# A macaron block (feed-forward, attention, feed-forward): the row maxima of head pairs 0 and 1 are found in one pass, pair 0 is attended two key blocks at a time, and some small steps change places

## The chip, the cores and the metric

The kernel runs on one core of a Trainium2 chip. The metric is the device time of one execution in microseconds (us). Below, PE is TensorE (matrix products), DVE is VectorE, ACT is ScalarE, POOL is GpSimd and SP is SyncE, whose queue issues the DMAs. PSUM, the memory that PE writes, has eight banks of 128 x 512 fp32 values.

## The reference

The input x has 2048 tokens of width 512. All products are in fp32.

```python
x = x + 0.5 * ffn(layernorm(x), gate, up, down)       # first feed-forward
x = x + attention(layernorm(x), w_qkv, w_out)         # 16 heads of 32, causal
x = x + 0.5 * ffn(layernorm(x), gate, up, down)       # second, with the same weights

# ffn:  W = LUT[4-bit code] * scale (4096 wide);  inter = gelu(x @ Wg.T) * (x @ Wu.T);  out = inter @ Wd.T
# attention, per head:  softmax(q @ k.T / sqrt(32) + causal mask) @ v;  then out @ w_out.T + b_out
```

## The kernel before, in words

The order of the work is written out by hand. Each engine carries out its instructions in the order in which the Python code emits them; semaphores between the engines follow from which tile each instruction reads and writes. PSUM is split into seven banks that are handed out as they come free (`ps_one`) and one for long accumulations (`ps_acc`). So a matrix product waits when its operand is late, or when no bank has been emptied.

The two feed-forward parts use Strassen-like schemes: seven products in place of eight, on sums of blocks, and in the second part a second level inside each. The first part dequantizes the weights and keeps them in DRAM; the second fetches them.

Attention works on pairs of heads. A head is 32 wide, so the queries and keys of four heads lie in one tile of 128 partitions, `qT` and `kT`: pair 0 in partitions 0 to 63, pair 1 in 64 to 127 (`quadrant`, which gives each head its 32 rows). A product of 32 rows uses a quarter of PE's rows, and products that lie in different quarters can run side by side.

A pair needs two passes. The first, `maxima(p)`, finds the largest score of each query, 40 steps of one 128-query tile against up to 512 keys (the last, diagonal, block of each tile is 128 to 512 wide). A step is one product per head (`pm`, L1208), and a reduction by DVE for each (L1220, or L1216 with the mask on a diagonal block). At the end of each group `g` of 512 queries the negated maxima are split into three bf16 parts by POOL (L1231) and turned into rows by PE (`row`, L1244), which ACT copies to `mrow` (L1245).

The second pass, `attend(p, width)`, again has 40 steps: 128 keys against 512 queries, or fewer on the diagonal. A step puts the maxima into a bank (`ps`, L1359, three bf16 rows), adds the scores of both heads (L1368), exponentiates them on ACT (L1393), and two steps later multiplies them with the values (`av`, L1280). The sums of each two steps' exponentials (L1417) are multiplied with ones to give the denominators, also at L1280. On a diagonal block DVE adds the mask to the first head's scores in PSUM (L1383); the second head's are copied out by ACT (L1386), masked by POOL (L1387) and exponentiated after that (L1395).

Normally `attend(p, 1)` runs in step with `maxima(p + 1)`: two heads' `ps` and the next pair's two `pm` fill the four quarters of PE. Two places are different. The maxima of pair 0 run before, with nothing beside them but the projections that fill the gaps (`pqk` L1124, `pv` L1141), one whole projection after every few steps. The last pair, 7, has no maxima behind it; its queries and keys are copied by DMA to the other half of the tile too, and `attend(7, 2)` takes two steps at once, one from each half, so that four `ps` run side by side.

While `attend(7)` runs, the layer norms for half of the second feed-forward are spread over its last group: `Norm(...).steps()` is a list of ten steps (two of moments on DVE, with the scales on POOL at the end of the second; four normalizations on DVE, L149; four transposes on PE, L155), and a tuple of numbers says after which of the 16 steps each is emitted.

The second feed-forward goes through 56 pairs of products for each half of the tokens (`pair`, seven slots each, L747), then the down products (`down`, `piece(i, q)`, L878): seven products `i` for each of two token groups `q`, slipped between the pairs. Products 1, 6, 7, 4 add up in one bank, 5 and 3 in another, 2 has its own; ACT takes a copy after 1, 6 and 5 (L901), and DVE adds the bank to the residual after the others (L887). Between the halves the class `Later` loads eight token tiles (`xl`, two buffers), normalizes them on ACT (L954), transposes them on PE (`pt_later`, L962) and copies them out. After the very last pair the remaining down products are emitted with the sums, gelus and gates that they need.

## Time and profile before

| | |
|---|---|
| median of 3 runs | 3151.17 us (3149.62 to 3152.65) |
| profiled execution | 3148.55 us; its span from first to last instruction 3146.7 us |
| PE busy | 3106.7 us, 99% of the span |
| DVE, ACT, POOL busy | 2054.1, 1046.7, 1532.9 us |
| last projections and tiles before the maxima of pair 0 | 1187.6 to 1203.4 us of the span |
| maxima of pair 0, with 12 projections between | 1203.4 to 1284.7 us |
| attention of pair 0 with the maxima of pair 1, and 8 projections | 1284.7 to 1385.2 us |
| attention of pair 7 (two steps at a time) | 1952.8 to 2037.1 us |
| last products | 3108.9 to 3142.8 us |

The profile's page gives busy shares by engine and slice, the chain of work that ended last, and groups of instructions by source line. In the timeline a row is: start, duration, engine, line, operation, output tile, input tiles, shapes, and xN for N equal instructions in a row; in brackets the idle time of the engine before it and what ended it. One fp32 product of the program is two matmuls of the profile.

### The profile page before, as it was taken

The page shows a single profiled execution, that of the slowest core. Times are in us where ns is not written, and L with a number is a line of the kernel's source. Part 1 is how long each engine was busy: PE and PEld are TensorE (multiplying, and loading weights), DVE is VectorE, ACT ScalarE, POOL GpSimd, SP SyncE. Part 2 cuts the span into 40 slices and gives each one's busy share as a digit, 9 for nine tenths or more (in the row PEclk, how much of TensorE's full clock was granted, in tenths as well). Part 3 has the DMA queues.
Part 4 walks back from the last instruction along what each step waited for, and adds up shares of the span by engine and source line. Part 5 has one row for each costly group of instructions (what it writes and reads, how often), then busy time and mean ns, then how long its engine had stood idle before and what let it go on. Part 6 is the DMA issues. An engine that isn't in the chain of part 4 may idle for free.

```text
span 3146.7 us, 45156 instructions
## 1 busy us (share of the span) xinstructions
PE 3106.7 (99%) x16592; PEld 2005.8 (64%) x16592; DVE 2054.1 (65%) x3182; ACT 1046.7 (33%) x2070; POOL 1532.9 (49%) x1529
## 2 busy tenths in 40 slices
PE   8999999999999999999999999999999999999999
PEld 4556565656555565444335434478888888888887
DVE  7566666666665655655564566687666777666676
ACT  5111111121111122355553456543333343333332
POOL 3757584857667572456664467522232223223221
PEclk9999999999999999999999999999999999999999
DMA  4223222212122220000000000064444445444442
GB/s 140 90 81 114 83 81 84 97 61 97 67 91 85 83 84 24 5 14 9 12 9 7 29 20 11 1 199 132 125 135 128 123 130 170 119 124 128 127 125 64
DMA packets 261293, 260.21 MB, mean 83 GB/s; under 512 B 21216, under 2 KB 225616, under 8 KB 257104
## 3 DMA queue, kind: packets, MB, share of 16 engines
q1 hardware_dynamic: 261072, 257.33, 25.2%
q8 instruction: 131, 2.15, 0.3%
q14 instruction: 90, 0.74, 0.1%
HBM read 176.28 MB, written 79.92 MB: 81 GB/s over the span
## 4 chain that ended last, share of the span: by engine, by line
PE 93%; DVE 3%; POOL 1%; ACT 1%; issue 1%; DMA 1%; SPq 0%; ACTq 0%; POOLq 0%; DVEq 0%
PE po L439 12%; PE pu L340 12%; PE d_f L747 12%; PE pg L340 12%; PE av L1280 7%; PE pod_f L878 7%; PE pm L1208 6%; PE f_f L747 6%; PE pqk L1124 4%; PE pof_f L878 3%; PE e_f L747 3%; PE ps L1359 2%; PE pv L1141 2%; PE pp L1161 2%; PE poe_f L878 2%; PE ps L1368 1%
## 5 line engine op out<-in xcount | busy, mean ns | idle before, releaser
L1393 ACT ACTIVATE pt<-ps 128x512 f32<-128x512 f32 (+3 forms) x608 | 288.1, 528 | 180.8 <-PE ps L1368 118.6
L1208 PE MATMUL pm<-kT,qT 32*128 32x512 f32 (+3 forms) x1280 | 332.4, 572 | 0.0
L1220 DVE TENSOR_REDUCE parts<-pm 128x1 f32<-128x512 f32 x384 | 246.5, 685 | 129.3 <-PE pm L1208 129.0
L747 PE MATMUL d_f<-ys_f,ring 128*128 128x256 f32 x1216 | 319.8, 384 | 6.1 <-DVE o_f L780 5.7
L1417 POOL TENSOR_TENSOR sum<-pt,pt 128x512 f32<-128x512 f32 (+1 forms) x225 | 265.6, 1200 | 95.6 <-ACT pt L1393 88.6
L1368 PE MATMUL ps<-qT,kT 32*128 32x512 f32 (+3 forms) x1280 | 278.3, 536 | 0.0
L747 PEld LDWEIGHTS d_f<-ys_f,ring 128*128 128x128 f32 x1216 | 227.1, 190 | 53.2 <-DVE o_f L780 21.3
L439 PEld LDWEIGHTS po<-wd,inter 128*128 128x128 f32 x1024 | 194.8, 190 | 77.2 <-issue 54.9
L801 DVE TENSOR_TENSOR o_f<-o_f,o_f 128x1024 f32<-128x1024 f32 x128 | 203.6, 1601 | 61.2 <-ACT o_f L786 56.5
L439 PE MATMUL po<-wd,inter 128*128 128x256 f32 x1024 | 241.1, 379 | 0.0
L340 PE MATMUL pg<-xT_f,w 128*128 128x512 f32 x512 | 239.1, 595 | 1.2 <-ACT u L379 1.2
L340 PE MATMUL pu<-xT_f,w 128*128 128x512 f32 x512 | 238.0, 593 | 0.0
L893 POOL TENSOR_TENSOR xq<-xq,d_f 128x512 f32<-128x512 f32 x48 | 63.6, 1324 | 311.2 <-DVE xq L887 230.3
L453 POOL TENSOR_TENSOR xq<-xq,d 128x512 f32<-128x512 f32 x124 | 161.9, 1316 | 92.0 <-DVE xq L447 55.8
L893 POOL TENSOR_TENSOR xq_second<-xq_second,d_f 128x512 f32<-128x512 f32 x45 | 61.5, 1367 | 277.2 <-DVE xq_second L887 212.3
L1280 PE MATMUL av<-pt,vals 128*32 128x256 f32 (+1 forms) x2432 | 191.5, 370 | 2.4 <-ACT both L1302 2.3
L439 PEld LDWEIGHTS po<-wd,s 128*128 128x128 f32 x768 | 145.7, 190 | 57.7 <-issue 38.9
L394 POOL TENSOR_TENSOR u<-u,u 128x512 f32<-128x512 f32 x64 | 81.7, 1277 | 206.7 <-ACT u L391 205.9
L439 PE MATMUL po<-wd,s 128*128 128x256 f32 x768 | 181.5, 379 | 0.0
L801 POOL TENSOR_TENSOR o_f<-o_f,o_f 128x1024 f32<-128x1024 f32 x44 | 119.2, 2709 | 123.9 <-ACT o_f L786 122.8
L340 PE MATMUL pg<-xsum,w 128*128 128x512 f32 x384 | 177.9, 592 | 0.0
L1280 PEld LDWEIGHTS av<-pt,vals 128*32 128x32 f32 x2432 | 53.0, 108 | 195.8 <-issue 167.9
(225 smaller groups left out, 6460.8 us busy)
## 6 DMA issues: line engine op xcount, KB each, us to landing
wd_f<-kept SPq DMA_DIRECT2D x112, 256.0 KB
kept<-wd SPq DMA_DIRECT2D x8, 1792.0 KB
xq<-in_x SPq DMA_DIRECT2D x16, 256.0 KB
pk<-in_gate_codes SPq DMA_DIRECT2D x16, 256.0 KB
sc<-in_gate_scales SPq DMA_DIRECT2D x32, 128.0 KB
pk<-in_up_codes SPq DMA_DIRECT2D x16, 256.0 KB
sc<-in_up_scales SPq DMA_DIRECT2D x32, 128.0 KB
pk<-in_down_codes SPq DMA_DIRECT2D x16, 256.0 KB
```

Source lines behind the costliest of these rows:

```text
L340: nc.tensor.matmul(ps, lhsT=a[:, j, :], rhs=b[:, j, :], start=(j == 0), stop=(j == 1))
L439: nc.tensor.matmul(ps[:, j, :], lhsT=a[i][:, k, bass.ts(2 * q + j, P)], rhs=b[i][:, k, :], start=(k == 0), stop=(k == 1),)
L453: adder.tensor_tensor(dst, dst, other, ALU.add)
L747: nc.tensor.matmul(ps[:, k, :], lhsT=fa[k][y], rhs=fb[k][y], start=first and k == 0, stop=True, skip_group_check=True,)
L801: sums.append(lambda: eng.tensor_tensor(dst, dst, other, ALU.add))
L878: nc.tensor.matmul(ps[:, j, :], lhsT=a[:, k, bass.ts(2 * q + j, P)], rhs=wd[:, PLACE[i], k, :], start=new and j == k == 0, stop=True, skip ...
L1208: nc.tensor.matmul(ps[a][:, :n], lhsT=q[r, bass.ts(4 * g + i, P)], rhs=k[r, kb * 512 : kb * 512 + n], start=True, stop=True,)
L1220: nc.vector.tensor_reduce(most, scores, AX.X, ALU.max)
L1280: nc.tensor.matmul(dst_, lhsT=lhsT, rhs=rhs, start=kw.get("start", False), stop=True, skip_group_check=True)
L1368: nc.tensor.matmul(ps[a][:, off:], lhsT=k[r, bass.ts(c, P)], rhs=q[r, g * 512 + off : (g + 1) * 512], start=False, stop=True,)
L1393: nc.scalar.activation(pt[:, a, plain[a] :], ps[a][:, plain[a] :], AF.Exp, scale=scale)
L1417: eng.tensor_tensor(s[:, a, off_2:], one[:, a, off_2:], other[:, a, off_2:], ALU.add)
```

## The change

Seven things, in the order of the code.

1. Last down products (`piece`, `down`, the end of `second_ffn`): for the last group, products 1 and 2 of both token groups come first, then 6, 5, 7, 3, 4 of each. For `q == 1` the copy after product 1 and the add after product 2 go; the bank is added to the residual at once. The sums, gelus and gates are placed anew between them: product 3 of the group before now follows product 5 directly.
2. `Later`: each transpose of the token tiles is emitted one slot earlier, with its load and the next normalization (the last transpose stays). One pair of sums in the second half moves one slot up.
3. `maxima(0)` and `maxima(1)` run zipped: a step has four `pm`, in four quarters, and four reductions. `split` has four buffers.
4. The fill is cut into units of one product (`pqk`) or a quarter of a `pv`; `take` says how many units follow a step. The prologue has two projections in place of four; the zipped pass takes all the rest and six of the eight projections of the second group of heads, and the last two are spread over `attend(0)`. Some of them use the free `ps_acc` bank. The bias of the values is added by ACT (copy) and POOL, and `kT` of the second group is written by ACT, both on DVE before.
5. Pair 0 joins pair 7 in `DOUBLE`: `attend(0, 2)` takes two steps at once. For that two DMAs copy pair 0's queries and keys into the other half of two spare tiles, and its maxima rows are made for both halves (eight transposes in place of four, two copies by ACT). Its divisions are done as pair 7's are (reciprocals on DVE, products on POOL, no DMAs), and the first head's half of each sum by DVE.
6. For both pairs in `DOUBLE` the mask of the second head's diagonal block is also added by DVE in PSUM, without the copy, the POOL mask and the extra exponential.
7. In `attend(7)` the second moments and scales of the second normed block are emitted after step 9 in place of 4, and its normalizations and transposes up to two steps later.

```diff
+DOUBLE = (0, NPAIR - 1)
 ...
-                orders = [(1, 2, 6, 5, 7, 3, 4)] * 2 if final else [DOWN, late]
+                order = [(i, q) for q, r in enumerate((DOWN, late)) for i in r]
+                if final:
+                    order = [(i, q) for i in (1, 2) for q in range(2)]
+                    order += [(i, q) for q in range(2) for i in (6, 5, 7, 3, 4)]
 ...
-                place = min(2 * i, 13)
-                at(0, 54 + place // 7, place % 7, call(later.transpose, i))
+                place = 53 * 7 + 6 + 2 * i
+                at(0, place // 7, place % 7, call(later.transpose, i))
 ...
-            at(1, 2, 3, *second[2:])
+            at(1, 2, 2, *second[2:])
 ...
-                    pieces.pop(0)()
-                    for f in sums:
-                        f()
-                    for piece in (pieces.pop(0), pieces.pop(1)):
-                        piece()
-                    for f in gelus + gated + down_sums[:2]:
-                        f()
-                    for piece in (pieces.pop(0), pieces.pop(0)):
-                        piece()
-                    for f in down_sums[2:]:
-                        f()
-                    for piece in pieces:
-                        piece()
+                    for part in (
+                        [pieces.pop(0)] + sums,
+                        [pieces.pop(0) for _ in range(3)] + gelus + gated,
+                        [pieces.pop(0)] + down_sums[:2],
+                        [pieces.pop(0) for _ in range(2)] + down_sums[2:],
+                        pieces,
+                    ):
+                        for f in part:
+                            f()
 ...
+            copies = [an.tile([P, S], F32, tag="attnT", name=f"copy{i}", bufs=3) for i in range(2)]
+            mcopy = [an.tile([P, D], F32, tag="xn", name=f"mcopy{i}").bitcast(BF16) for i in range(2)]
 ...
-                        for i in range(2):
-                            nc.vector.tensor_tensor(
-                                vals[...], ps[:, i, :], bv_sb[...], ALU.add)
+                        if half == 0:
+                            nc.scalar.copy(both, ps[0])
+                        for i in range(2):
+                            eng, src = (nc.gpsimd, both) if half == 0 else (nc.vector, ps[0])
+                            eng.tensor_tensor(both[:, i, :], src[:, i, :], bv_sb[...], ALU.add)
 ...
-                                halves = (p % 2,) if p + 1 < NPAIR else (0, 1)
+                                halves = (0, 1) if p in DOUBLE else (p % 2,)
 ...
+                            for a in range(2 if p in DOUBLE else 1):
+                                own = ps[a][:, off : off + P]
+                                nc.vector.tensor_tensor(own, own, mask_k, ALU.add)
+                            if p not in DOUBLE:
+                                plain[1] = off + P
+                                ...
 ...
-            for piece in qk[:4]:
+            for piece in joined(qk[:2]):
                 piece()
                 for step in norms[:3]:
                     step()
                 del norms[:3]
-            fill = qk[4:6] + v[:2] + qk[6:8] + v[2:]
-            for n, (matmuls, rest, diagonal) in enumerate(maxima(0)):
+            def second_group():
+                nc.sync.dma_start(out=wqk_sb, in_=wqk[1])
+                for src, dst in zip((qT, kT), copies):
+                    nc.sync.dma_start(out=dst[64:, :], in_=src[0][:64, :])
+            for piece in qk[2:6] + v[:2] + qk[6:] + [second_group] + v[2:] + following[:6]:
+                ...

+            for n, pair in enumerate(zip(maxima(0), maxima(1))):
                 for a in range(2):
-                    matmuls(a)
+                    for matmuls, _, _ in pair:
+                        matmuls(a)
                 for a in range(2):
-                    rest(a, now)
+                    for _, rest, _ in pair:
+                        rest(a, now)
                 now += 1
+                take = 3 if n < 3 else 4 if n == 39 else 1 if n in (10, 11, 22, 23, 32) else 2
+                for f in units[:take]:
+                    f()
 ...
-                0: lambda: spread(project_qk(1)),
+                0: lambda: [[], following[6], following[7], []],
 ...
-                            after = ((0, 1, 4, 5, 6, 6, 7, 8, 9, 10), (3, 4, 9, 10, 11, 12, 12, 13, 14, 15))[tb][i]
+                            after = ((0, 1, 4, 5, 6, 6, 7, 8, 9, 10), (3, 9, 11, 11, 12, 12, 13, 13, 14, 15))[tb][i]
 ...
-                ahead = maxima(p + 1) if p + 1 < NPAIR else iter(())
+                ahead = iter(()) if p in DOUBLE else maxima(p + 1)
 ...
-                for steps in attend(p, 2 if p + 1 == NPAIR else 1):
+                for steps in attend(p, 2 if p in DOUBLE else 1):
```

## The prediction

> **What bounds the kernel now.** I read the page first, then the timeline of PE from the last projections to the end of pair 7, then the waits of PE in the stages that the diff touches.
>
> ```profile
> PE 3106.7 (99%) x16592; PEld 2005.8 (64%) x16592; DVE 2054.1 (65%) x3182; ACT 1046.7 (33%) x2070; POOL 1532.9 (49%) x1529
> ...
> 1209.83 1.13 PE L1208 MATMUL pm<-kT,qT 32*128 32x512 f32 x4
> 1210.89 3.70 PE L1124 MATMUL pqk<-xT_a,wqk_wv 128*128 128x512 f32 x8
> ...
> 1324.75 0.39 PE L1359 MATMUL ps<-wo_bo,ones_b 3*128 3x512 bf16 x1
> 1324.75 0.69 PE L1208 MATMUL pm<-kT,qT 32*128 32x512 f32 x1
> ...
> 1325.93 0.64 PE L1280 MATMUL av<-pt,vals 128*32 128x256 f32 x8
> 1326.50 0.39 PE L1359 MATMUL ps<-wo_bo,ones_b 3*128 3x512 bf16 x1
> ...
> 1982.05 0.40 PE L1359 MATMUL ps<-wo_bo,ones_b 3*128 3x512 bf16 x4
> 1982.28 1.03 PE L1368 MATMUL ps<-qT,kT 32*128 32x512 f32 x8
> 1983.23 0.64 PE L1280 MATMUL av<-pt,vals 128*32 128x256 f32 x8
> 1983.69 0.61 PE L1280 MATMUL av<-sum,ones_f 128*32 128x256 f32 x8
> 1984.12 0.61 PE L1280 MATMUL av<-pt,vals 128*32 128x256 f32 x8
> 1984.67 0.40 PE L1359 MATMUL ps<-wo_bo,ones_b 3*128 3x512 bf16 x4
> ```
>
> PE is the bound nearly everywhere, so a gain is either PE time that goes or one of its few waits. But busy isn't full: from start to start, a step of `pm` takes 1.06 us (1209.83 to 1210.89) with two of four quarters in use, and a step of pair 0's attention beside `pm` 1.18 + 0.57 us (1324.75, 1325.93, 1326.50). Pair 7's double step of four `ps` takes the same 1.18 us (1982.05 to 1983.23) for two steps' scores, and 2.62 us in all. So half of PE is unused in the maxima of pair 0, and the last pair shows what filling it gives.
>
> ```profile
> PE pt_f L155 <- ACT xn_f L146: 11.6, 4, 8.7
> PE d_f L747 <- DVE o_f L780: 5.7, 5, 2.3
> PE ps L1359 <- ACT pt L1393: 3.3, 3, 2.0
> PE pt_later L962 <- ACT xl L954: 2.9, 5, 1.4
> ...
> 2015.86 0.75 PE L155 MATMUL pt_f<-ident,xn_f 128*128 128x128 f32 x4 [1.30 <-DVE xn_f L149]
> 2019.31 0.26 PE L1359 MATMUL ps<-wo_bo,ones_b 3*128 3x128 bf16 x1 [1.98 <-ACT pt L1393]
> 2020.47 1.08 PE L1280 MATMUL av<-pt,vals 128*32 128x256 f32 x8
> ```
>
> These are PE's waits (total, times, longest): the 3.3 us and the two rows below lie in pair 7, the 2.9 us between the halves of the second feed-forward; the first row is the kernel's start, which stays. In the last row the same `av` that took 0.64 us takes 1.08: the granted clock is 0.88 in the 20 us from 2020.
>
> **The change part by part.** Built, both programs have the same PE products except 16 more row transposes; the PE sum is about which run side by side.
>
> *Attention of pair 0.* Two full steps are 1.75 and 2.22 us now (1324.75, 1326.50, 1328.72), 3.97 together, against 2.62 for a double step: 1.35 saved, 12 times. For the diagonal the timeline gives 2.21 + 1.49 against 2.61 (512 and 384 wide) and 1.66 + 1.01 against 2.09: 1.09 and 0.58, four times each. Together 16.2 + 4.4 + 2.3 = 22.9 us. The projections (8 x 3.63 us) and the rows of pair 1 (4 x 0.34) only move into the stage before.
>
> *Maxima of pairs 0 and 1.* Pair 1's `pm` go into the two free quarters. Price: 1.06 us a full step as now, if four overlap as two do. Pair 7's four fp32 `ps` take 0.95 us after their bf16 rows, so I take 0 for that. Here a rule speaks against the change. The Trainium skill, "TensorE: Matmul & The Clock Gate", in "Part 3: Packing small matmuls", gives four row tiles of 32 x 512 a measured speedup of 3.07, not 4. By the rule a full step's 0.855 us of streaming (1242.96 to 1245.73 is three steps, less 0.2 of entry) would become 1.11, over 24 full and 16 partial steps (34 in full widths) an estimated +8.8 us. The row of this trace is the nearer case; I keep 0, and 8.8 as the other end. What does cost is that now every step stands between fills: 19 blocks of `pm` today become 40, and each entry from a 128-row product costs 1.06 - 0.855 = 0.2 us, so 21 x 0.2 = +4.3 us.
>
> *Who keeps up.* PE in the new stage: 80 units x 0.907 = 72.6, `pm` 28 x 1.06 + 4 x (0.85 + 0.63 + 0.42) = 37.3, seven tile transposes x 0.63 and six row groups x 0.34 = 6.4, in all 116 us. DVE: 96 reductions at 0.635 (eight in 5.08 us) = 61, diagonals 16 x (0.645 + 0.515 + 0.385 + 0.25) = 29, moments and small ones 5, in all 95 us; that is why the bias of the values and `kT` leave it. Per full step it is 2.54 against 2.88 us. ACT gets 14 x 0.59 for projections, 8 x 0.57 for values, POOL 16 x 0.77 for the bias (the 128x256 row of L272) beside 16 x 1.26 of residual bias: both under half. Banks: four `pm`, at times an open projection. When the next step starts 2.9 us later, DVE has emptied two or three, so four are free. The cover goes once: the moments of the second normed block (4 x 0.8 us) now stand on DVE after the third step and, behind them, a reciprocal that waits for ACT; the next step's reductions queue behind it, and the fourth `pm` of the first full step waits for its bank, 1.5 us. Also the first `pm` waits for `kT` off ACT (0.59 us, partly under a transpose): 0.4. Today's 0.9 us of waits for `xn_a` there go.
>
> *Start of pair 0's attention.* Nothing is pending, no projection stands in its first group, and the first values wait for masks (4 x 0.25) and exponentials (2.1 us): 2 us of idle PE, bounds 1 and 3.5. Afterwards ACT has 2.1 us per double step of 2.62; 1 us more for odd waits. SP: reloading the weights waits for the last old projection, and the two copies (0.5 MB each) stand behind it. Their reader is some 60 us away and nothing else is in SP's queue there; 38 DMAs net go with pair 0's divisions. Cost 0.
>
> Front sum: -22.9 + 4.3 + 1.5 + 0.4 - 0.9 + 2 + 1 = -14.6 us.
>
> *Pair 7.* Now POOL's mask for the second head stood behind POOL's divisions, sums and `rstd`: ACT's copy at 2012.3 is masked at 2018.1, and ACT, held by it, empties no banks: PE waits 1.98. In the second group of queries the same chain seems to cost 1.19 (1973.13). Both go with the DVE mask; 1.30 and 0.16 go as the second block's moments (1.6 us) no longer stand between the first two normalizations. From 2019.3 to 2024.25 PE needs 4.93 us for what takes 2.64 elsewhere: 2.3 us of clock. Sum 4.8 + 2.3 = 7.1. New: 16 more masks of 0.25 us on DVE (busy 49 of the stage's 84 us), and the banks of the 384-wide step still come free about 1 us late; the later moments are wanted 1.6 us after they end. I take -6, ends 0 and -7.5. The second rule weighed is about this clock. The same page, "Part 1: The HAM clock gate", halves the clock after an idle window of about 3.4 us. Here the clock fell with no single wait above 1.98 us. By the rule alone the 2.3 us would not be blamed on these waits (-3.7), and 2 us at pair 0's start would be safe; by the row, waits close together suffice. I go with the row.
>
> *Between the halves.* The third tile's load is issued before SP's queue takes the next weight fetch, not behind it (both second loads leave only at 2546.51 now), and the last normalization stands one slot ahead of its transpose (1.39 of the 2.9 us). I take -2, ends -3 and 0. The moved pair of sums swaps with a gate sum on a busy DVE: 0.
>
> *Last products.* PE's waits after the last pair are 1.08, 1.67 and 1.02 us, all for DVE's gates and sums. The order 4, 5, 1, 3, 2, 6, 5 becomes 4, 5, 3, 1, 1, 2, 2, 6, 5 (two token groups of 1 and 2), which gives DVE 3.45 us more before 6. New: product 3 directly after 5 waits for ACT's copy, 0.2 + 0.6 = 0.85 us, and DVE takes product 3's bank before the gates, +0.6. Then 6 is nearly in time (0.1), and 5 waits 1.0 as now: 3.77 - 1.95 = -1.8, with the gaps from start to start somewhat more; -2, ends -3 and +1.
>
> Total: -14.6 - 6 - 2 - 2 = -24.6 us. Against its own time, 3148.55 - 24.6 = 3124. The shown median is 2.6 above that execution, so 3127.
>
> **The rivals.**
>
> *The zipped stage is held by banks and DVE.* If a step's four banks come free only behind DVE, a full step takes 2.54 + 0.9 = 3.4 instead of 2.88 us; over 28 steps +14, so 3141. For it: seven banks, four taken at once, and ACT's share of the emptying. Against: DVE's 95 us in 116.
>
> *Pair 0's double steps are held by ACT.* At 2.1 us of exponentials plus masks and copies in a chain, 0.4 us more per double step is +8: 3135. Against: pair 7 shows 2.62 without a wait in its third group, though there projections give ACT time.
>
> *Four `pm` don't overlap.* Then pair 1's two follow pair 0's with an entry of their own, 1.06 us again for a full step, 37.3 us over the stage: -24.6 + 37.3 = +12.7, slower than before, 3164. It decides from 24.6 / 34 = 0.72 us more per full width. Against: the four `ps` at 0.95 us. For it: no row shows four fp32 products right after 128-row ones, with four loads of weights to enter.
>
> *The edits of parts 7, 2 and 1 do nothing* (each wait is replaced by another): 3137.
>
> **How the numbers follow.** Sum as worked out, 3119 to 3133: 0.63. Banks or ACT or no gain at the end, 3133 to 3144: 0.29. Four `pm` one pair after the other: 0.05. Some unseen wait that eats the gain to within 0.2%: 0.03. The point is 3127. To hold 8 in 10, I take 3119 to 3140. A measurement tells 0.2% (6.3 us) from no change: faster 0.92, same 0.03, slower 0.05.
>
> **What would show it.** After: `pm` rows of x8 in about 1.06 us between fills; the zipped stage about 118 us long with DVE four fifths busy; pair 0's attention near 58 us; `ps` in pair 7 without waits for ACT above 1 us and a clock of 1.00; waits of `pt_later` under 1 us. I am wrong if a `pm` x8 row takes 1.3 us or more, if PE waits for DVE at each step of the zipped stage, or if the clock drops at the start of pair 0's attention.

## The result, and the profile after

The changed kernel takes 3135.74 us (median, 3131.5 to 3136.55) beside 3151.02 us before on the same chip: a ratio of 0.9954, 95% interval 0.9942 to 0.9966. The forecast was 3127 (3119 to 3140) and faster; the gain is 15 us where the sum said 24.6.

The profiled execution takes 3135.08 us, its span 3133.2. By stages (the borders are the first instruction of each on PE):

| stage | before | forecast | after |
|---|---|---|---|
| last projections, maxima of pair 0 (after: of 0 and 1), attention of pair 0 | 197.6 us | -14.6 | 187.6 us (7.8 + 121.0 + 58.8) |
| pairs 1 to 6 | 567.6 | 0 | 566.6 |
| attention of pair 7, to the second feed-forward | 94.7 | -6 | 91.8 |
| second feed-forward to the last gate product | 1060.4 | -2 | 1060.6 |
| from there to the last product's end | 35.0 | -2 | 34.0 |

The start of the kernel, before all this, was 0.9 us longer in this execution (PE waits 12.5 us for ACT's first normalizations, 11.6 before), and 0.3 us went after the last product: -10.1 - 1.0 - 2.9 + 0.2 - 1.1 + 0.9 + 0.3 = -13.7, the difference of the spans (-13.6) but for rounding. The 1.0 us of pairs 1 to 6 lies in pair 1's first steps, from which, among others, the last rows of its maxima (0.34 us) have moved forward.

PE's waits after (total, times, longest):

```profile
PE pt_f L156 <- ACT xn_f L147: 12.5, 4, 9.6
...
PE ps L1403 <- ACT pt L1439: 2.3, 4, 1.4
...
PE pt_later L970 <- ACT xl L962: 1.6, 3, 0.6
...
PE pm L1248 <- ACT kT L1152: 0.3, 1, 0.3
```

Of pair 7's 1.98 and 1.19 us for ACT 0.28 is left in the `ps` row; the longest wait of that row, 1.4 us, is new and stands at the start of pair 0's attention. `pt_later` went from 2.9 to 1.6 us. The zipped stage has one wait, 0.3 us for `kT`.

The timeline of PE in the zipped stage:

```profile
1210.99 1.93 PE L1248 MATMUL pm<-kT,qT 32*128 32x512 f32 x8
...
1239.84 1.98 PE L1146 MATMUL pqk<-xT_a,wqk_wv 128*128 128x512 f32 x4
...
1257.40 1.14 PE L1248 MATMUL pm<-kT,qT 32*128 32x512 f32 x8
1258.48 1.99 PE L1175 MATMUL pv<-wqk_wv,xT_a 128*128 128x256 f32 x8
...
1313.70 3.70 PE L1146 MATMUL pqk<-xT_a,wqk_wv 128*128 128x512 f32 x8
1317.33 0.38 PE L1403 MATMUL ps<-wo_bo,ones_b 3*128 3x512 bf16 x1
```

A `pm` row of x8, four quarters, takes 1.08 us from start to start (1257.40 to 1258.48), as x4 took 1.06 before. A block of four fill matmuls (two products) takes 1.91 to 1.92 us (the one at 1239.84 ends with the next row's start at 1241.75), a block of eight 3.63 (1313.70 to 1317.33, where the first `ps` starts). The first full step (1210.99, to 1212.86) takes 1.87: 0.8 us of waiting for a bank, which the records show as a longer row. Then the start of pair 0's attention, which waits for the first exponentials:

```profile
1318.42 0.28 PE L1403 MATMUL ps<-wo_bo,ones_b 3*128 3x256 bf16 x2
1320.09 0.21 PE L1403 MATMUL ps<-mcopy,ones_b 3*128 3x128 bf16 x1 [1.39 <-ACT pt L1439]
```

Pair 7, where the clock fell, and the same place with the granted clock (a row of the second view: stretch, its length, busy us of PE, PEld, DVE, ACT and POOL with counts, clock, DMA):

```profile
2002.53 0.74 PE L156 MATMUL pt_f<-ident,xn_f 128*128 128x128 f32 x4 [0.51 <-DVE xn_f L150]
2003.94 0.74 PE L156 MATMUL pt_f<-ident,xn_f 128*128 128x128 f32 x4 [0.66 <-DVE xn_f L150]
...
2005.32 0.64 PE L1403 MATMUL ps<-wo_bo,ones_b 3*128 3x256 bf16 x2 [0.28 <-ACT pt L1439]
...
2006.87 1.08 PE L1323 MATMUL av<-pt,vals 128*32 128x256 f32 x8
```

```profile
2001.93:2005.34 3.41, 1.96 (x15) 1.31 (x12) 3.20 (x7) 1.16 (x3) 2.56 (x4) 1.00 0.01 2
2005.34:2008.75 3.41, 3.39 (x30) 1.57 (x33) 1.72 (x7) 2.66 (x8) 0.99 (x1) 0.50 0.02 5
2008.75:2012.16 3.41, 3.41 (x28) 1.42 (x20) 1.82 (x5) 0.59 (x1) 1.27 (x2) 0.50 0.00 0
```

The waits for ACT are 0.28 us now, but two of 0.51 and 0.66 for the normalizations stand there, and `av` still takes 1.08 us in place of 0.64: for 6.8 us the clock is exactly half, with PE busy again. So the 2.3 us of clock that I had counted as gained were not gained here. (The stretch from 2005.34 is busy for 3.39 of 3.41 us, and the next one is at half clock all the same.)

The last products on PE before, of which only the last gate product and product 5 are shown, then after, and DVE beside them:

```profile
3107.91 1.13 PE L747 MATMUL d_f<-ys_f,ring 128*128 128x256 f32 x4
...
3123.69 2.00 PE L878 MATMUL pof_f<-wd_f,inter_f 128*128 128x256 f32 x8 [1.02 <-DVE inter_f L859]
```

```profile
3095.09 1.13 PE L748 MATMUL d_f<-ys_f,ring 128*128 128x256 f32 x4
...
3100.36 1.99 PE L879 MATMUL pof_f<-wd_f,s_f 128*128 128x256 f32 x8 [0.69 <-ACT d_f L904]
...
3110.20 1.97 PE L879 MATMUL pod_f<-wd_f,s_f 128*128 128x256 f32 x8 [0.35 <-issue]
3113.25 1.99 PE L879 MATMUL pof_f<-wd_f,inter_f 128*128 128x256 f32 x8 [1.09 <-DVE inter_f L860]
```

```profile
3102.77 1.22 DVE L802 TENSOR_TENSOR o_f<-o_f,o_f 128x1024 f32<-128x1024 f32 x1
3103.92 0.68 DVE L888 SCALAR_TENSOR_TENSOR xq_second<-pof_f,xq_second 128x512 f32<-128x512 f32 x1
3105.33 1.77 DVE L814 TENSOR_TENSOR inter_f<-o_f 128x512 f32<-128x512 f32 x2 [0.73 <-ACT o_f L805]
```

The three waits before product 5 (1.08, 1.67, 1.02) are four now, 0.69, 0.31, 0.35 and 1.09. DVE stands 0.73 us for ACT's gelus between product 3's add (3103.92) and the gates.

### The profile page after: what moved, and what is told of

Read it like the earlier page. It is cut to its first block, busy times and chain, and to the rows that moved or that the text cites. A ratio compares the mean times of both kernels' runs of the same rounds, so it can differ in the third digit from the quotient of the medians.

```text
span 3133.2 us, 45074 instructions
## 1 busy us (share of the span) xinstructions
PE 3096.3 (99%) x16608; PEld 1995.8 (64%) x16608; DVE 2069.6 (66%) x3217; ACT 1043.0 (33%) x2029; POOL 1521.9 (49%) x1512
## 4 chain that ended last, share of the span: by engine, by line
PE 94%; DVE 2%; ACT 1%; issue 1%; POOL 1%; DMA 0%; SPq 0%; POOLq 0%; ACTq 0%; DVEq 0%
PE po L440 12%; PE d_f L748 12%; PE pu L341 12%; PE pg L341 12%; PE av L1323 7%; PE pod_f L879 7%; PE pm L1248 6%; PE f_f L748 6%; PE pqk L1146 4%; PE pof_f L879 3%; PE e_f L748 3%; PE ps L1403 2%; PE pp L1201 2%; PE pv L1175 2%; PE ps L1412 2%; PE poe_f L879 1%
## 5 line engine op out<-in xcount | busy, mean ns | idle before, releaser
L1463 POOL TENSOR_TENSOR sum<-pt,pt 128x512 f32<-128x512 f32 (+1 forms) x210 | 249.2, 1205 | 121.2 <-ACT pt L1439 99.1
L1248 PE MATMUL pm<-kT,qT 32*128 32x512 f32 (+3 forms) x1280 | 297.2, 576 | 0.3 <-ACT kT L1152 0.3
L1412 PE MATMUL ps<-qT,kT 32*128 32x512 f32 (+3 forms) x1200 | 261.2, 539 | 0.0
L341 PE MATMUL pu<-xsum,w 128*128 128x512 f32 x384 | 177.7, 592 | 0.0
```

Of the source, the lines that this page charges most:

```text
L341: nc.tensor.matmul(ps, lhsT=a[:, j, :], rhs=b[:, j, :], start=(j == 0), stop=(j == 1))
L1248: nc.tensor.matmul(ps[a][:, :n], lhsT=q[r, bass.ts(4 * g + i, P)], rhs=k[r, kb * 512 : kb * 512 + n], start=True, stop=True,)
L1412: nc.tensor.matmul(ps[a][:, off:], lhsT=k[r, bass.ts(c, P)], rhs=q[r, g * 512 + off : (g + 1) * 512], start=False, stop=True,)
L1463: eng.tensor_tensor(s[:, a, off_2:], one[:, a, off_2:], other[:, a, off_2:], ALU.add)
```

## The experiments

### The front alone

The kernel before with parts 3 to 5, and the DVE mask for pair 0 only (against the changed kernel; parts 1, 2 and 7 are as before):

```diff
-                            for a in range(2 if p in DOUBLE else 1):
+                            for a in range(2 if p == 0 else 1):
 ...
-                            if p not in DOUBLE:
+                            if p != 0:
```

> The kernel before with the zipped maxima and pair 0's double steps alone (parts 3 to 5, and the DVE mask for pair 0 only); pair 7, the token tiles between the halves and the last products stay as before. If the stages add up as the trace of the changed kernel shows them, the front (from the last projections to the end of pair 0's attention) takes 187.6 us instead of 197.6 and the kernel is 10 to 11 us faster, 3140 to 3141. If part of the gain came from an interplay with the other parts, it is less than 8. My forecast of -14.6 for the front would give 3136.5. Pair 7 should look as before: a wait of about 2 us of the scores for ACT, and the clock at half for some us after it; if the clock falls by chance, pair 7 may be without it.

Measured: 3139.81 us beside 3149.92, ratio 0.9963 (0.995 to 0.9977): 10.1 us, as expected. By stages 7.81 + 120.98 + 58.76 us in front, to 0.02 us what the changed kernel shows, and 35.0 for the last products. Pair 7 took 93.95 us, with the waits of 1.30 and 1.99, but this time the clock was half for 3.4 us only. So the front stands by itself, is worth 10 to 11 us, and my 14.6 was wrong in the front itself.

### Mask, token tiles and last products without the norms; the norms alone

Two kernels split what I had put into one sum for pair 7. Each ran once. The first has parts 1 and 2 besides the cut shown here.

```diff
+                            for a in range(2 if p + 1 == NPAIR else 1):
+                                own = ps[a][:, off : off + P]
+                                nc.vector.tensor_tensor(own, own, mask_k, ALU.add)
+                            if p + 1 < NPAIR:
 ...
```

> The kernel before with three edits that lie far apart, so that the trace can be read stage by stage: the second head's mask on DVE in pair 7 (part 6, without the new places of the norms), the token tiles one slot earlier (part 2) and the last products in the new order (part 1). Pair 7: if the mask alone was behind the waits, the 1.98 and 1.19 us for ACT go and 1.30 + 0.16 for the normalizations stay or grow, since DVE now also carries 16 masks: 84.4 + 1 to -3.3 us; if the new places of the norms are needed as well, pair 7 is not shorter than 93.8 us up to the first gate product. Token tiles: -1.5 us as in the changed kernel. Tail: -1.1 us as there (waits of 2.4 us in place of 3.8). Whole kernel 3144 to 3149.

```diff
-  (3, 4, 9, 10, 11, 12, 12, 13, 14, 15)
+  (3, 9, 11, 11, 12, 12, 13, 13, 14, 15)
```

> The kernel before with the new places of the second block's moments and normalizations in pair 7 alone (part 7, without the mask on DVE). By my sum the waits of 1.30 and 0.16 us for the normalizations go and the 1.98 and 1.19 us for ACT stay, since POOL's mask is still there: pair 7 takes 93.2 us in place of 94.7, plus or minus 2 us for where the clock falls. If the order of the norms on DVE was what held POOL's mask too, the 1.98 us go as well and pair 7 takes 91 us or less. Outside pair 7 nothing changes: front 197.6 us, last products 35.0 us.

The first took 3141.51 us, with pair 7 at 89.1 us, both below what was expected, in a trace in which the clock stayed up; the second 3147.98, pair 7 at 93.4, as expected. Their timelines of PE in pair 7's last group, the mask alone first:

```profile
2015.29 0.75 PE L155 MATMUL pt_f<-ident,xn_f 128*128 128x128 f32 x4 [1.30 <-DVE xn_f L149]
...
2016.67 0.59 PE L1362 MATMUL ps<-wo_bo,ones_b 3*128 3x256 bf16 x2 [0.28 <-ACT pt L1397]
...
2017.69 0.64 PE L1283 MATMUL av<-pt,vals 128*32 128x256 f32 x8
```

```profile
2014.32 1.34 PE L155 MATMUL pt_f<-ident,xn_f 128*128 128x128 f32 x8 [0.17 <-DVE xn_f L149]
...
2018.39 0.26 PE L1359 MATMUL ps<-wo_bo,ones_b 3*128 3x128 bf16 x1 [2.00 <-ACT pt L1393]
...
2019.55 1.08 PE L1280 MATMUL av<-pt,vals 128*32 128x256 f32 x8
```

With the mask alone the waits for ACT are gone (0.28 is left of 1.98, and in the second group the 1.19 too), those for the normalizations stay (0.16 and 1.30), and the clock doesn't fall: `av` 0.64. With the norms alone it is the other way round: 0.17 is left of 1.46, 2.00 stays, and `av` is at 1.08. The forecast's two causes of the waits are as it had them, one for each edit; what the clock follows, one execution of each doesn't show. In the mask kernel the token tiles and the last products show what the changed kernel showed: 1059.0 us in place of 1060.4 in the second feed-forward, 33.95 in place of 35.0 at the end.

### What the fill's blocks cost

The zipped stage was 3 us longer than my sum. A block of eight matmuls costs 3.63 us and two of four 3.83; so each block costs 0.2 us of its own beyond 0.43 per matmul. I had costed the 80 units at 0.907 us, a quarter of a block of eight, and so had 20 entries in the sum; the stage has 40 blocks. To see whether that time can be had back:

```diff
+                if n >= 12:
+                    take = (2 if n == 22 else 3 if n == 32 else 6 if n == 38 else 4) if n % 2 == 0 else 0
                 for f in units[:take]:
```

> The changed kernel with the fill of the zipped maxima in blocks of four units after every second step from step 12 on, 14 blocks in place of 28. If each block costs an entry of its own and nothing else binds (0.19 us into 128 rows, 0.2 us back), the stage goes from 121.0 to 115.5 us and the kernel to 3130. If banks are the limit once two steps stand side by side (eight products for seven banks, each freed by a reduction of 0.64 us), the second step of each pair loses 0.4 to 1.1 us, the stage takes 121 to 131 us and the kernel 3136 to 3145. I expect the second, about +3 us; the trace then still shows the x8 blocks of fill at 3.63 us against twice 1.91.

Measured: 3144.85 us beside 3149.92, ratio 0.9984 (0.9977 to 0.999), 9 us slower than the changed kernel where I had expected 3. The zipped stage takes 132.7 us in place of 121.0, pair 0's attention 62.5 in place of 58.8. Of these 3.7 us 0.6 are waits (2.6 in place of 2.0, of which 1.2 for DVE's reductions, since the stage inherits full banks); the rest fits the clock, which was half from 1331.75 to 1338.58 in this trace.

```profile
1248.64 3.03 PE L1248 MATMUL pm<-kT,qT 32*128 32x512 f32 x16
1251.59 3.72 PE L1175 MATMUL pv<-wqk_wv,xT_a 128*128 128x256 f32 x16
1255.24 3.62 PE L1248 MATMUL pm<-kT,qT 32*128 32x512 f32 x16
1258.80 3.72 PE L1175 MATMUL pv<-wqk_wv,xT_a 128*128 128x256 f32 x16
```

The fill's own block of x16 (256 wide, as much as x8 of 512) takes 3.65 us (1251.59 to 1255.24) where two blocks take 3.84: the entry is real. But two steps side by side take 2.95 and 3.56 us here in place of twice 1.08. That fits their eight products, which want eight banks where seven are handed out: DVE's first reduction behind the row at 1248.64 starts at 1249.80. So the rival of the banks was right about the resource and wrong about the change as made: with two units of fill behind each step the banks come free in time. The 0.2 us for each block is the price of that, and blocks twice as long don't win it back here.

### What a pause of PE does to its clock

The clock fell in pair 7 for 6.8, 3.4 or 0 us in traces in which the code of pair 7 is one and the same. This kernel puts pauses of known length into the second feed-forward of the three-places kernel (below):

```diff
+            def there_and_back(hops):
+                for _ in range(hops):
+                    pt = ps_one.tile([P, P], F32, tag="one", name=f"pt_pad_{next(serial)}")
+                    nc.tensor.transpose(pt, pad, ident)
+                    nc.scalar.copy(pad, pt)
+
+            for i in range(25):
+                at(0, 4 + 2 * i, 3, call(there_and_back, 3 + i % 5))
```

> What a pause of PE does to its clock, measured by itself: the three-places kernel with 25 pauses in the first half of the second feed-forward, some 19 us apart, each a chain of 3 to 7 transposes of a tile of zeros with an ACT copy between each two (their result is not used). One step of a chain is about 0.5 us from the like rows (copy of a bank 0.6 us for four times the width, a release about 0.2), so the pauses are about 1 to 3 us, and the kernel some 60 us longer. If the clock is decided at the edges of a free-running grid of about 3.4 us by the busy share of the last stretch (what the falls in the traces so far look like: edges 2005.2, 2012.1, 2589.0, 2592.4), then falls begin at whole multiples of 3.41 us from each other, last 3.4 or 6.8 us, follow pauses of 3 us nearly always, of 2 us sometimes and of 1 us never. If only an idle stretch of 3.4 us halves the clock, none of these pauses does. If falls are chance, they don't follow the length of the pause.

It ran once and takes 3226.67 us, 102 us more than without the pauses (60 expected). A step of a chain is 0.69 us, about half of it idle; the pauses hold 1.1, 1.4, 1.8, 2.2 and 2.5 us of idle PE. One of six steps, and the granted clock there and at a shorter pause; after these, the clock at a single wait of 2.26 us for DVE in the changed kernel and in the second trace of the three-places kernel:

```profile
2113.27 0.33 PE L991 MATMUL pt_pad<-ident,pad 128*128 128x128 f32 x1 [0.73 <-ACT pad L992]
...
2116.01 0.33 PE L991 MATMUL pt_pad<-ident,pad 128*128 128x128 f32 x1 [0.36 <-ACT pad L992]
2116.18 3.08 PE L879 MATMUL pod_f<-wd_f,inter_f 128*128 128x256 f32 x8
```

```profile
2113.32:2116.73 3.41, 1.98 (x8) 1.17 (x9) 3.38 (x5) 1.42 (x6) 0.00 (x0) 1.00 0.08 20
2116.73:2120.14 3.41, 3.41 (x10) 2.69 (x9) 0.69 (x2) 0.96 (x2) 0.00 (x0) 0.50 0.30 105
2120.14:2123.55 3.41, 3.41 (x17) 3.00 (x17) 2.58 (x4) 0.31 (x1) 0.00 (x0) 1.00 0.00 0
...
2164.52:2167.93 3.41, 2.32 (x12) 1.63 (x11) 3.41 (x4) 1.28 (x4) 0.00 (x0) 1.00 0.81 247
```

```profile
2585.60:2589.02 3.42, 1.23 (x6) 1.10 (x7) 3.42 (x6) 0.06 (x1) 0.00 (x0) 1.00 0.00 0
```

```profile
2579.91:2583.32 3.41, 1.61 (x7) 1.44 (x8) 3.41 (x6) 0.45 (x1) 0.00 (x0) 1.00 0.00 0
```

After 13 of the 25 pauses the clock was half: after none of the five with 3 steps, none with 4, three with 5, all with 6 and with 7. The 13 falls begin at whole multiples of 3.413 us from each other (0, 7.00, 14.00, 34.00, 41.00, 49.00, ... 151.00 of them over 515 us), and last one such stretch (11 times) or two (2 times). Cut along this grid, the stretch before a fall at a pause has PE busy for 0.39 to 0.59 of its time, and every other stretch among the pauses that began at full clock 0.66 or more. After a fall the clock came back behind a stretch with PE busy for 0.89 or more, and stayed half behind 0.80 and 0.86.

So the fall is neither chance alone nor a matter of one long wait: it goes with what PE does in a stretch of 3.41 us whose borders the kernel doesn't choose. In the changed kernel the two falls, at 2005.34 and 2589.02, are 171.0 stretches apart.

But the busy share of the profile is not the measure. The wait of 2.26 us for DVE near the start of the second half, among long products, stands in all twelve traces, the one before the change too. Where it left one stretch 0.36 (changed kernel, above) or 0.34 busy (the ladder, 173.0 stretches behind its first fall) the clock fell. In the other ten it left 0.47 (three places, above) to 0.65 in its emptier stretch, and nothing fell, nor behind a stretch of 0.46 in the last products of the kernel before (3116.91 to 3120.32). The ladder's pauses fell at up to 0.59, but part of that is single transposes of 0.33 us each. Without these the falls at its pauses stand at 0.26 or less and its other stretches at 0.36 or more, close to the limit of the long products. So it fits all of this that a lone transpose counts for little; no run singles it out. Among the short products of pair 7 stretches of 0.65, 0.66, 0.68 and 0.69 were followed by a fall, while one of 0.57 (the front alone, from 2001.08) and one of 0.59 (the mask alone, from 2011.82) were not. What the gate counts there no trace says.

### The last products, two single edits

```diff
-                        [pieces.pop(0) for _ in range(3)] + gelus + gated,
+                        [pieces.pop(0)] + gelus,
+                        [pieces.pop(0) for _ in range(2)] + gated,
```

> The changed kernel with one edit in the last products: ACT's two gelus are emitted before its copy of product 1, all products and DVE's work in the same order. In the changed kernel DVE waits 0.73 us for the gelus behind that copy, and the first gates, product 2, 6 and 5 are all late by it. If this is the part of my sum that failed, the stretch from the last gate product to the end takes 33.2 to 33.3 us in place of 34.0 (product 3's wait of 0.7 us stays); if DVE's adds are the limit, it stays at 34.0. Also a second look at pair 7 of the changed kernel: 87.7 us where the clock stays up, 90 to 92 where it falls.

```diff
-                        [pieces.pop(0)] + sums,
-                        [pieces.pop(0) for _ in range(3)] + gelus + gated,
+                        [pieces.pop(0)] + sums,
+                        [pieces.pop(0), pieces.pop(1), pieces.pop(0)] + gelus + gated,
```

> The changed kernel with one edit in the last products: product 3 stands behind the first product 1, so that it no longer waits 0.7 us for ACT's copy of product 5. By my prediction's sum that wait was worth its 0.7 us: the stretch would take 33.3 us in place of 34.0. If DVE's chain of gates and sums sets when product 5 may start, the 0.7 us come back as longer waits of products 2, 6 and 5 and it stays at 34.0. Also a third look at pair 7 of the changed kernel.

Each ran once, and both give 33.74 us in place of 33.97: 0.2 each, not 0.7. With the gelus first DVE no longer stands before the gates, but the pair of gates takes 2.36 us, 1.77 in the changed kernel. What is beside it on DVE and on POOL:

```profile
3103.22 0.68 DVE L888 SCALAR_TENSOR_TENSOR xq_second<-pof_f,xq_second 128x512 f32<-128x512 f32 x1
3103.82 2.36 DVE L814 TENSOR_TENSOR inter_f<-o_f 128x512 f32<-128x512 f32 x2
```

```profile
3103.98 1.65 POOL L894 TENSOR_TENSOR xq_second<-xq_second,d_f 128x512 f32<-128x512 f32 x1 [3.02 <-DVE xq_second L888]
```

DVE's add of product 3 (3103.22) releases POOL's add to the same tile at 3103.98, and while that runs, to 3105.63, the second gate doesn't get on: the first takes 0.68, the second ends only at 3106.18, about 0.6 behind POOL's end. In the changed kernel POOL's add (3104.68, 1.27 us) lies partly behind the wait for the gelus and partly in the first gate; so to take the wait away only shows the add. The Trainium skill, "SBUF — State Buffer", "Who interferes with whom", has it as a rule: a DVE instruction with two inputs in SBUF contends with a POOL instruction that reads SBUF, the shared ports are an exclusive lock, and the order of issue decides who waits. The gates are of that kind, and the rows agree.

With product 3 later, PE's 0.69 us are gone and come back as a wait of product 6:

```profile
3098.30 1.89 PE L879 MATMUL pof_f<-wd_f,s_f 128*128 128x256 f32 x8
...
3107.01 1.97 PE L879 MATMUL pod_f<-wd_f,s_f 128*128 128x256 f32 x8 [1.43 <-issue]
3110.07 1.99 PE L879 MATMUL pof_f<-wd_f,inter_f 128*128 128x256 f32 x8 [1.09 <-DVE inter_f L860]
```

Product 5 starts when DVE's chain has come to its operand, and PE's waits before it only say where PE stands meanwhile. Pair 7 took 90.5 us in both kernels (one stretch of half clock each), and in the first the clock fell for 3.41 us at the start of pair 0's attention too (from 1320.73, behind the 1.39 us wait there), and that stage took 1.5 us more (60.3).

### Three places, and both kernels once more

What the trace of the changed kernel showed late, each with one edit: (a) two of pair 7's last projections stand before its first transposes, where PE waits; (b) pair 0's two projections come one group earlier, over the 1.39 us; (c) DVE's gates and the first three sums come before its four adds.

```diff
-                        extra.setdefault(STARTS[3] + i, []).append(o3[4 + i])
+                        extra.setdefault(STARTS[3] + (0, 1, 6, 7)[i], []).append(o3[4 + i])
 ...
-                0: lambda: [[], following[6], following[7], []],
+                0: lambda: [following[6], following[7], [], []],
 ...
-                        [pieces.pop(0) for _ in range(3)] + gelus + gated,
-                        [pieces.pop(0)] + down_sums[:2],
-                        [pieces.pop(0) for _ in range(2)] + down_sums[2:],
+                        [pieces.pop(0)] + gelus,
+                        [pieces.pop(1)] + gated + down_sums[:3],
+                        [pieces.pop(0) for _ in range(4)] + down_sums[3:],
```

> The changed kernel with three edits from what its trace shows: two of pair 7's last projections stand before the first transposes (where PE waits 0.51 and 0.66 us and the clock falls), in place of two steps that had work enough; the two projections in pair 0's attention stand in groups 0 and 1, not 1 and 2; in the last products gelus, gates and the first three sums come before the adds of product 3 and 1 on DVE, and ACT's gelus before its copy of product 1. Expected: pair 7 -1.2 us for the waits, and -3 more if the fall of the clock follows PE's idle share (if it falls by chance or from the short products alone, it stays); start of pair 0's attention -1 us (0 if the extra bank makes the scores wait); tail -2.7 us (0 if DVE's chain of sums and gates is not what product 5 waits for). Sum -8, 3128; 3134 if only the waits of pair 7 go.

Measured: 3124.53 us beside 3149.92, ratio 0.9919 (0.9906 to 0.9933). Its timeline in the three places:

```profile
1318.42 1.98 PE L1146 MATMUL pqk<-xT_a,wqk_wv 128*128 128x512 f32 x4
1320.34 0.28 PE L1403 MATMUL ps<-wo_bo,ones_b 3*128 3x256 bf16 x1
```

```profile
2000.66 1.02 PE L1201 MATMUL pp<-wo_bo,attnT 128*128 128x512 f32 x2
2001.52 0.63 PE L156 MATMUL pt_f<-ident,xn_f 128*128 128x128 f32 x4
...
2002.83 0.64 PE L1323 MATMUL av<-pt,vals 128*32 128x256 f32 x8
```

```profile
3100.22 1.89 PE L879 MATMUL pod_f<-wd_f,s_f 128*128 128x256 f32 x8
3101.94 1.89 PE L879 MATMUL pof_f<-wd_f,inter_f 128*128 128x256 f32 x8
```

(a) Transposes without a wait, `av` at 0.64, pair 7 86.9 us in place of 91.8; (b) 1.92 us of projection stand where PE had waited 1.39, and the stage takes 57.4 us in place of 58.8; (c) product 5 directly behind 6, and the stretch 30.6 us in place of 34.0: the gates take 1.47 us, since POOL's add comes behind them now. Together 9.6 us, and the fall at 2589 (1.7 us) wasn't there this time. New is a wait of 0.4 us in pair 7, for a bank that one of DVE's adds holds.

> The changed kernel unchanged, once more, beside the three-places kernel on the same chip. The front and the last products should repeat to 0.1 us (7.8, 121.0, 58.8 and 34.0). If the fall of the clock is decided by where a free-running grid of 3.41 us falls on PE's waits, the grid stands at another place in this execution: pair 7 takes 87.7 to 88.8 us without a fall, about 90.5 with one stretch and 91.8 with two, and the start of the second half (2.3 us wait) has one or none; whole kernel 3131 to 3137. If the fall belonged to the code, pair 7 would take 91.8 again.

> The three-places kernel once more, beside the changed one: 57.4, 86.9 and 30.6 us for pair 0's attention, pair 7 and the last products, without a fall of the clock in pair 7 whatever the place of the grid (its waits there are gone). Ratio to the kernel before 0.992, and 8 to 11 us under the changed kernel.

On one chip: the changed kernel 3134.26 us, ratio 0.9952 (0.9937 to 0.9967); the three places 3124.77, ratio 0.9924 (0.9907 to 0.994), 9.5 us under it. The front repeated (7.81, 120.98, 58.76), pair 7 of the changed kernel took 90.4 us with one stretch of half clock (2006.79 to 2010.20), and the three-places kernel 86.9 again without one. This kernel is faster than both that the document began with.

## Why the prediction was right and wrong

Right in direction, and in range; the point was 8.7 us too fast. By its steps:

- *Attention of pair 0, -22.9, +2 at its start, +1 of odd waits.* Holds. Without projections and rows the stage went from 100.5 - 29.0 - 1.4 = 70.1 us to 58.8 - 7.7 - 0.6 = 50.5: -19.6 against -19.9. PE stood idle 2.1 us, 1.39 of it at the start; "near 58" was 58.8. The sign of being wrong "if the clock drops at the start of pair 0's attention" didn't show in this trace, but did in one of five with this front (gelus first) and in the blocks of four: 2 us of idle PE there were not always safe.
- *Maxima of pairs 0 and 1, 0 for the overlap.* Holds: 1.08 us with four quarters against 1.06 with two. The row of pair 7's `ps` that I took in place of the 3.07 of the Trainium skill ("TensorE: Matmul & The Clock Gate", Part 3) was the right one; by my estimate from the page the rows would have been 0.25 us longer. So the rival "four `pm` don't overlap" falls.
- *Entries, +4.3.* This is the term that was mis-sized. I counted 0.2 us for each entry from a 128-row product into `pm`, but not that the way back is entered as often, at 0.19 us for each of 40 blocks. From the row of 3.63 for eight matmuls the fill's 80 units were 72.6 us, with 20 such entries in them; they are 160 matmuls x 0.43 + 40 x 0.19 = 76.4, and the trace has 76.36. That is +3.8 of the 4.6 us by which the front missed, and the size of the stage: 116 forecast with 1.9 of waits, 121.0 measured. The trace of before had it to be read: a projection of eight matmuls behind a transpose takes 3.43 us there (1194.97 to 1198.40), behind a step of `pm` 3.63 (1210.89 to 1214.52).
- *Who keeps up.* Holds, and the blocks of four show how near the edge it is. The waits for banks at the first full step (1.5 forecast) were 0.8, 0.4 and 0.1 at three steps; that for `kT` was 0.3 (0.4 forecast). DVE was busy 94.4 us of 121 (95 forecast). The rival "held by banks and DVE" falls for the change as made, and so does "held by ACT": ACT was busy 41.7 of 58.8 us.
- *Pair 7, -6.* The two causes are as forecast, each shown alone: 1.98 and 1.19 go by the mask, 1.30 by the norms. But "1.30 and 0.16 go" doesn't hold in the changed kernel: 0.51 + 0.66 = 1.17 of the 1.46 us are there in four of five traces, since DVE's first two normalizations take 2.09 us there and 1.28 in the fifth. Why they do is likely POOL (last section), and stays open. The clock is the other step that failed: "I go with the row" was to say that the fall belongs to these waits and leaves with them. It leaves with them only if nothing like them is left, and 0.51 + 0.66 + 0.28 us are left beside each other: in all four traces with these three waits the clock fell, in the three of the three-places pair 7, which has one wait of 0.4 us, it did not, nor in the blocks of four, with 0.17 and 0.28. In five traces of this code pair 7 took 91.8, 90.5, 90.5, 90.4 and 87.7 us, -2.9 to -7.0 of the before trace's 94.7. The bounds of 0 and -7.5 hold, and -6 lies near the lucky end. The rule that I weighed against the row ("Part 1: The HAM clock gate" of the same page) has the window, 3413 ns and free-running, as the grid shows it, and an idle window as the condition, which the traces don't bear out: a stretch with PE busy for 0.34 or 0.36 of it was enough among long products. Row and rule were each half right.
- *Between the halves, -2.* -1.5 from the start of the second feed-forward to behind the transposes (13.05 to 14.55 us ahead of the kernel before), and the 1.7 us that the clock took at 2589 hid it in the profiled execution. `pt_later` still waits 1.6 us, where under 1 was forecast. In the other traces with this edit the stage takes 1059.0 to 1060.2 us, in those without it 1060.1 to 1060.6.
- *Last products, -2.* -1.07. The term that was mis-sized is DVE's chain. I gave it +0.6 for product 3's bank; from the last gate product to product 5's operand it became 2.4 us longer (15.8 to 18.2): two adds more stand in it, of the second product 1 and the second product 2 (0.6 each; product 3's add, for which I had put the +0.6, stood in it before too), and for the rest DVE waits 0.73 for the gelus behind a copy of product 1, and POOL's add costs the gates 0.3. PE got two products more in front of it, 3.45 us, so 3.45 - 2.4 = 1.1. Edit (c) shows it: with adds and copy behind the chain the same products end 3.3 us earlier. The gelus alone were not the term: with them first the stretch lost only 0.2 us.

Two rivals come near in time, "ACT holds the double steps" with 3135 and "parts 7, 2 and 1 do nothing" with 3137, and both are wrong in mechanism: the double steps are as forecast, each of the three parts gave something, and the front gave less by its blocks of fill.

## What to carry to other kernels

Where work of a few rows and work of all rows take turns on PE, count an entry in both directions for every change between them, and read it from blocks of two lengths (3.63 against 1.91 us here). A pause of PE costs its length and, where it falls so in the grid of 3.4 us that PE does too little in one stretch, up to 1.7 or 3.4 us more by half clock; where the grid falls differs between executions. So several short waits close together can cost more than their sum, and in pair 7 a projection or two moved between them took away both. Where PE waits for the end of a chain on another engine, moving products on PE only moves the wait; take from the chain what needn't be in it.

## What the runs showed of the hardware

- The clock of PE changes on a grid of 3.413 us that runs through the whole execution (falls 2589.02 - 2005.34 = 171.0 stretches apart), to half exactly, for one or two stretches. Among long products with one wait a stretch with PE busy for 0.34 or 0.36 was followed by half clock, 0.46 and more was not. With short products the busy time of the profile doesn't order the cases: in pair 7 falls behind 0.37 to 0.69, none behind a stretch of 0.57 and one of 0.59.
- Four fp32 products of 32 x 512 in four quarters take 1.08 us where two take 1.06.
- DVE and POOL hold each other up: the pair of gates took 1.47 us without POOL beside it and 2.36 with POOL's add (128x512), a sum of 128x1024 took 1.22 and 1.98. In pair 7 the same two normalizations (`xn_f`, 128x512) took 2.09 us in the changed kernel's trace and 1.28 in that of the blocks of four, between the same instructions of POOL, and with them PE's waits 0.51 + 0.66 or 0.17; the second of them started 0.12 us behind a sum of POOL there (2002.39, 2002.27) and ended 0.28 behind its end, while in the blocks of four it started before that sum (2017.20, 2017.66). That this too is a matter of who comes first is likely, and no run here singles it out.
